# A two-layer graph network on one core: small loads moved to GpSimd's queue, and the order of the first and last pairs laid anew

## The chip, the cores and the metric

The kernel runs on one core of a Trainium2 chip. The core has five engines with a queue of instructions each: TensorE (PE, matrix products), VectorE (DVE), ScalarE (ACT), GpSimd (POOL) and SyncE (SP, which here only issues transfers). The time is device microseconds of one execution; the median of the runs before is 2428.2 us (three runs, 2427.8 to 2429.03). Profiled executions are recorded engine by engine, with the TensorE clock that was granted (1.00 is full speed).

## The reference

x is 128 images (graphs) of 128 nodes with 512 features, float32; adj is one 128 x 128 matrix of zeros and ones for all of them.

```python
def _L0_gnn_ref(x, adj, Wq, bq, Wk, bk, Wv, bv, Wo, bo):      # 8 heads of 64
    q = (x @ Wq + bq).reshape(b, n, H, HD)                    # k and v likewise
    scores = einsum('bqhd,bkhd->bhqk', q, k) / sqrt(HD)
    scores = scores + (1.0 - adj)[None, None, :, :] * -1000000000.0
    attn = softmax(scores, axis=-1)
    out = einsum('bhqk,bkhd->bqhd', attn, v).reshape(b, n, d)
    return out @ Wo + bo

def _L1_gnn_ref(x, W, a, beta, mask):
    h = einsum('bnc,cf->bnf', x, W)
    s1 = einsum('bnf,f->bn', h, a1); s2 = einsum('bnf,f->bn', h, a2)
    e = leaky_relu(s1[:, :, None] + s2[:, None, :], 0.2) * mask[None, :, :]
    att = softmax(e, axis=2)
    return elu(einsum('bij,bjf->bif', att, h) + beta * h)

x = layernorm(x + _L0_gnn_ref(x, adj, ...))
x = layernorm(x + _L1_gnn_ref(x, W, a, beta, adj))
```

## The kernel before

**Pairs.** The 128 images are worked on two at a time, 64 pairs (`G = 2`, `NG = 64`). For each pair the two images are the columns of one 2 x 2 block product: q, k, v, the output product w and the product h of the second layer are each formed by seven block products instead of eight (`product(name, g, n)` with n from 1 to 7), from sums of blocks of the weights (`weight_sum`, formed once at the start) and of the data (`block_sum`, on GpSimd for each pair). Products 1 and 2 need plain blocks alone; the others need sums. A product of q or k is four matmuls of 128 x 128, one of v, w or h two of 128 x 256; as float32 each matmul stands in the trace as two passes. Partial results are taken from PSUM by ScalarE (`take_part`, `take_block`, with the bias `bq_c` or `bk_c`) and by VectorE (`add_block`).

**Stages of a pair.** `fetch_blocks` loads x in blocks (tile xblk, four transfers of 32 partitions), `turn_x` transposes it on VectorE into xT, `block_sum` makes tx; then the products of q and k, `scores` on TensorE, `mask` and `row_max` on VectorE, `exps` and `normalise` on ScalarE. The attention weights are written to DRAM and read back in another layout (`attn_write`, `attn_read`, both on SyncE's queue) and transposed on VectorE (`turn_attn`); then `attend` with v, the product w, to which x + bo is added (`fetch_x`, `residual` on GpSimd), the normalisation, the small attention of the second layer, the product h, elu, the second normalisation and `store`. For the last pair the products w and h are plain ones (`plain`), for which the upper halves of wo and w1 are loaded again into the tiles of wq and wk (`load_again`).

**The order.** Nothing is scheduled automatically. Each step is entered with a number, its place (`at(place, fn, ...)`); all steps are sorted by place and issued in that order (the last three lines of the function). Places of a pair are relative to `g * STEP`, with `STEP = 37.33`; `rows(g)` lists the steps with their usual places, `other` replaces the places of pairs 0 to 3 and of three of the last ones, and `last_rows(g)` has the last pair's own list. The steps that are run once (`weight_sum`, `make_mask`, `make_beta`, `wa_column`, `wa_turn`, `wa_centre`, the loads of wo and w1) have places of their own at the end. An engine works through its instructions in the order of the places, and waits for whatever an instruction needs.

**The loads at the start.** What is issued before the sorted steps stands at lines 119 to 159: four transfers of pair 0's xblk and four of wq, two of each on SyncE's and two on ScalarE's queue; four of wk and four of wv on SyncE's; then eight small ones on ScalarE's queue: the columns bq_c, bk_c and bv_c (128 partitions x 4 single elements), adj, beta broadcast to all partitions, the two halves of a1 broadcast (tile uf, 128 x 512) and bo broadcast (128 x 512). Afterwards `make_identity` builds ident on GpSimd, and `keep_busy(20, "early")` issues 20 matmuls of ident with itself, whose result nobody reads.

**Completion counters.** Transfers issued by SyncE and ScalarE take turns on eight completion counters; a transfer whose counter was used before waits, on its queue, until the transfer that used it last has landed. Transfers issued by GpSimd have eight counters of their own; the kernel before issues none there.

**Who needs what.** The table load ahead of ScalarE's first eviction, and the eviction, need bq; `make_mask` needs adj; `wa_column(j, c)` multiplies a block of w1 by a half of a1 (VectorE, eight of them), from which `wa_turn` and `wa_centre` make two rows that `row_product` uses; `residual` needs bo; `attend_evict` needs bv.

Of the kernel before, what the change touches and what calls it, by code (L numbers as in the profile page):

```python
# [8 lines left out]
F32 = mybir.dt.float32  # L9
AF = mybir.ActivationFunctionType  # L10
ALU = mybir.AluOpType
AX = mybir.AxisListType

P = 128
# [4 lines left out]
STEP = 37.33  # L19
# [3 lines left out]
def gnn_two_layers(  # L23
# [34 lines left out]
    nc = tc.nc  # L58
# [49 lines left out]

    def broadcast(pool, src, n, name):
        t = pool.tile([P, n], F32, tag=name, name=f"{name}_in")  # L110
        nc.scalar.dma_start(out=t, in_=src.rearrange("(o n) -> o n", o=1).broadcast_to([P, n]))
        return t

    def column(src, name):
        t = cpool.tile([P, NC], F32, tag=name, name=name)
        nc.scalar.dma_start(out=t, in_=src.rearrange("(c p) -> p c", p=P))
        return t
# [6 lines left out]
    bq_c = column(bq, "bq_c")  # L124
    bk_c = column(bk, "bk_c")
    adj_sb = cpool.tile([P, N], F32, tag="adj_sb", name="adj_sb")
    nc.scalar.dma_start(out=adj_sb, in_=adj)
    bv_c = column(bv, "bv_c")
    beta_b = broadcast(cpool, beta, 1, "beta_b")
    a_b = [  # L130
        broadcast(wk2, a1[j * D : (j + 1) * D].rearrange("f o -> (f o)"), D, "uf")
        for j in range(2)
    ]
    bo_b = broadcast(cpool, bo, D, "bo_b")
# [24 lines left out]
    nc.gpsimd.memset(mhalf, -0.5)  # L159

# [8 lines left out]
    def make_beta():  # L169
        nc.vector.tensor_scalar(beta_i, ident, beta_b, None, ALU.mult)  # L170
# [6 lines left out]
    def wa_column(j, c):  # L177
        t = wk2.tile([P, D], F32, tag="u", name=f"wa_t_{j}_{c}", bufs=1)
        nc.vector.scalar_tensor_tensor(
            t, w1_sb[:, c, :], 1.0, a_b[j], ALU.mult, ALU.mult,  # L180
            accum_out=wa_col[:, j, c : c + 1],
        )
# [255 lines left out]
    def residual(b):  # L438

        xr[b] = xn.pop(b)  # L440
        nc.gpsimd.tensor_tensor(xr[b], xr[b], bo_b, ALU.add)  # L441
# [25 lines left out]
    def attend_evict(b):  # L467

        oT[b] = wk2.tile([P, NC, N], F32, tag="oT", name=f"oT_{b}")
        nc.vector.tensor_tensor(  # L470
            oT[b], po.pop(b),
            bv_c.rearrange("p (m o) -> p m o", o=1).broadcast_to([P, NC, N]), ALU.add,
        )
# [247 lines left out]
    def last_rows(g):  # L721
        b0, b1 = g * G, g * G + 1
        return (
            (-59.639, fetch_blocks, g), (-24.809, turn_x, g, 0), (-24.149, turn_x, g, 1),
            (-23.429, product, "q", g, 1), (-23.349, block_sum, "x", g, 1),
            (-22.314, take_part, "q", g, 1, 0, 0), (-19.649, block_sum, "x", g, 2),
            (-18.909, block_sum, "x", g, 4), (-18.469, fetch_x, b0),
            (-18.169, block_sum, "x", g, 3), (-18.019, fetch_x, b1),
            (-16.444, product, "q", g, 2), (-15.549, product, "q", g, 7),
            (-15.019, residual, b0), (-14.924, add_block, "q", g, 0, 0, 2, 1),  # L730
            (-14.654, product, "k", g, 7), (-12.889, product, "k", g, 1),
            (-11.994, product, "k", g, 2), (-10.519, take_part, "k", g, 1, 0, 0),
            (-9.799, residual, b1), (-9.379, add_block, "k", g, 0, 0, 2, 1),
            (-9.359, product, "q", g, 6), (-8.244, take_part, "q", g, 6, 1, 0),
            (-8.214, product, "k", g, 6), (-7.319, product, "q", g, 5),
            (-6.769, take_part, "k", g, 6, 1, 0), (-6.109, take_part, "q", g, 5, 1, 1),
            (-5.554, product, "k", g, 5), (-4.649, add_block, "q", g, 1, 1, 7, 5),
            (-3.789, product, "q", g, 4), (-3.349, take_part, "k", g, 5, 1, 1),
            (-2.894, product, "q", g, 3), (-2.649, add_block, "q", g, 1, 0, 4, 6),
            (-2.229, add_block, "k", g, 1, 1, 7, 5), (-1.999, product, "k", g, 3),  # L740
            (-1.779, take_block, "q", g, 0, 1), (-1.104, product, "k", g, 4),
            (-0.884, take_block, "k", g, 0, 1), (0.011, add_block, "k", g, 1, 0, 4, 6),
            (0.661, scores, b0), (1.781, product, "v", g, 1), (2.001, mask, b0, 0),
            (2.671, mask, b0, 1), (2.871, take_part, "v", g, 1, 0, 0), (3.341, row_max, b0),
            (4.201, scores, b1), (4.801, exps, b0, 0), (5.441, mask, b1, 0),
            (5.591, exps, b0, 1), (6.111, mask, b1, 1), (6.781, row_max, b1),
            (6.971, exps, b0, 2), (7.761, exps, b0, 3), (8.691, row_inv, b0),
            (9.141, exps, b1, 0), (9.551, product, "v", g, 7), (9.931, normalise, b0, 0),
            (10.531, normalise, b0, 1), (11.131, normalise, b0, 2), (11.291, product, "v", g, 2),
            (11.731, normalise, b0, 3), (12.381, add_block, "v", g, 0, 0, 2, 1),  # L750
            (12.471, attn_write, b0), (13.891, exps, b1, 1), (14.681, exps, b1, 2),
            (15.471, exps, b1, 3), (15.621, attn_read, b0), (15.641, product, "v", g, 6),
            (16.661, row_inv, b1), (16.731, take_part, "v", g, 6, 1, 0),
            (17.111, normalise, b1, 0), (17.381, product, "v", g, 5), (18.091, normalise, b1, 1),
            (18.691, take_part, "v", g, 5, 1, 1), (19.071, normalise, b1, 2),
            (19.581, add_block, "v", g, 1, 1, 7, 5), (19.671, normalise, b1, 3),
            (19.991, product, "v", g, 3), (20.001, turn_attn, b0, 0), (20.411, attn_write, b1),
            (20.861, product, "v", g, 4), (21.081, take_block, "v", g, 0, 1),
            (21.081, turn_attn, b0, 1), (22.441, add_block, "v", g, 1, 0, 4, 6),
            (23.001, attend, b0), (23.561, attn_read, b1), (25.321, attend_evict, b0),  # L760
            (26.141, plain, "w", b0), (27.801, turn_attn, b1, 0), (29.291, turn_attn, b1, 1),
            (29.951, plain_take, b0), (30.091, attend, b1), (31.301, attend_evict, b1),
            (32.801, plain, "w", b1), (33.361, row_product, b0, 0), (34.091, row_product, b0, 1),
            (34.821, bn_stats, y, b0, "c"), (35.511, bn_aggr, b0, "c"),
            (35.711, add_eps, g, "c", 0), (36.301, inv_std, g, "c", 0), (37.141, plain_take, b1),
            (37.801, scale_s, g, 0), (37.971, bn_stats, y, b1, "c"), (38.861, bn_aggr, b1, "c"),
            (39.061, add_eps, g, "c", 1), (39.231, row_product, b1, 0),
            (39.731, spread_s2, g, 0), (39.961, inv_std, g, "c", 1), (40.381, edge, g, 0),
            (40.711, norm_c, b0), (41.241, row_product, b1, 1), (41.971, scale_s, g, 1),
            (42.141, leaky, g, 0), (42.411, edge_max, g, 0), (42.681, norm_c, b1),  # L770
            (42.821, edge_exp, g, 0), (43.021, spread_s2, g, 1), (43.221, keep_busy, 6, "late"),
            (43.631, edge, g, 1), (43.961, leaky, g, 1), (44.231, edge_max, g, 1),
            (44.501, edge_inv, g, 0), (44.641, edge_exp, g, 1), (44.671, weights, g, 0),
            (45.391, turn_weights, g, 0), (45.691, edge_inv, g, 1),
            (45.811, weights_evict, g, 0), (45.861, weights, g, 1), (46.331, turn_weights, g, 1),
            (46.531, aggregate, b0), (46.751, weights_evict, g, 1), (47.451, aggregate, b1),
            (48.041, aggregate_evict, b0), (48.631, aggregate_evict, b1),
            (48.771, plain, "h", b0), (52.221, plain, "h", b1), (52.771, elu_exp, b0),
            (55.511, elu_max, b0), (55.891, elu_exp, b1), (56.201, elu_sum, b0),
            (56.891, elu_max, b1), (57.581, bn_stats, u, b0, "f"), (58.271, elu_sum, b1),  # L780
            (58.961, bn_aggr, b0, "f"), (59.161, add_eps, g, "f", 0),
            (59.331, bn_stats, u, b1, "f"), (59.471, inv_std, g, "f", 0),
            (60.021, bn_aggr, b1, "f"), (60.221, add_eps, g, "f", 1), (60.391, shift, g, 0),
            (60.531, inv_std, g, "f", 1), (60.731, norm_f, b0), (61.411, shift, g, 1),
            (61.651, store, b0), (61.751, norm_f, b1), (62.671, store, b1),
        )
# [5 lines left out]
            3.605, 8.805, 9.465, 11.005, 14.385, 10.265, 15.125, 11.405, 13.415, 16.725, 12.3,  # L792
# [204 lines left out]
```

## Time and profile before

| | us |
|---|---|
| median of three runs | 2428.2 |
| the profiled execution | 2425.9 |
| its span in the trace | 2424.1 |
| first slice of 40 (60.6 us): busy TensorE / VectorE / ScalarE / GpSimd, tenths | 7 / 4 / 3 / 4 |
| TensorE without work from 60 to 320 us | 4.6 |
| the same from 320 to 2280 us | 1.4 |
| the same from 2280 to 2386 us | 2.5 |
| the same from 2386 us to the end, 2424.1 | 10.2 |
| last matmul ends at | 2415.6 |

The page gives for each engine its busy time and its share of the span; the order of time of an engine gives start and duration of groups of instructions, and in brackets how long the engine was idle before and what ended that. `SPq` and `ACTq` are the issues of transfers on a queue. A view by windows gives, for each stretch of time, the busy time of each engine, the granted clock, the busy share of the 16 DMA engines and the rate. Between 320 and 2280 us a pair takes 36.98 us, and TensorE has work nearly all the time. The loads of the first 60 us, with their size and the time from issue to landing:

```profile
wk_sb<-in_L_gnn_Wk_dram SPq DMA_DIRECT2D x4, 256.0 KB, 7.6
wv_sb<-in_L_gnn_Wv_dram SPq DMA_DIRECT2D x4, 256.0 KB, 9.3
w_sb<-in_L_gnn_W_dram SPq DMA_DIRECT2D x1, 1024.0 KB, 8.8
wo_sb<-in_L_gnn_Wo_dram SPq DMA_DIRECT2D x1, 1024.0 KB, 11.3
uf_in<-in_L_gnn_a_dram ACTq DMA_DIRECT2D x2, 256.0 KB, 5.5
bo_b_in<-in_L_gnn_bo_dram ACTq DMA_DIRECT2D x1, 256.0 KB, 8.4
adj_sb<-in_adj_dram ACTq DMA_DIRECT2D x1, 64.0 KB, 7.3
bq_c<-in_L_gnn_bq_dram ACTq DMA_DIRECT2D x1, 2.0 KB, 8.5
bk_c<-in_L_gnn_bk_dram ACTq DMA_DIRECT2D x1, 2.0 KB, 7.6
```

### The profile page before, as it was taken

The page shows a single profiled execution, that of the slowest core. Times are in us where ns is not written, and L with a number is a line of the kernel's source. Part 1 is how long each engine was busy: PE and PEld are TensorE (multiplying, and loading weights), DVE is VectorE, ACT ScalarE, POOL GpSimd, SP SyncE. Part 2 cuts the span into 40 slices and gives each one's busy share as a digit, 9 for nine tenths or more (in the row PEclk, how much of TensorE's full clock was granted, in tenths as well). Part 3 has the DMA queues.
Part 4 walks back from the last instruction along what each step waited for, and adds up shares of the span by engine and source line. Part 5 has one row for each costly group of instructions (what it writes and reads, how often), then busy time and mean ns, then how long its engine had stood idle before and what let it go on. Part 6 is the DMA issues. An engine that isn't in the chain of part 4 may idle for free.

```text
span 2424.1 us, 50042 instructions
## 1 busy us (share of the span) xinstructions
PE 2389.7 (99%) x17956; PEld 2205.0 (91%) x17956; DVE 1912.0 (79%) x4385; ACT 1488.4 (61%) x5310; POOL 854.8 (35%) x1037
## 2 busy tenths in 40 slices
PE   7999999999999999999999999999999999999998
PEld 6998999999999999999999999999999999999985
DVE  4787787787877877878878778778778787787787
ACT  3665656656666566566566665665665666656655
POOL 4333323423333333234233333332342333333322
PEclk8999999999999999999999999999999999999999
DMA  6324234233242342342332433423424324334331
GB/s 162 119 74 114 79 105 120 75 112 105 82 119 93 92 123 80 105 121 73 113 104 81 122 93 91 123 80 105 119 75 113 106 79 122 92 92 123 88 105 70
DMA packets 204536, 245.30 MB, mean 101 GB/s; under 512 B 20480, under 2 KB 151680, under 8 KB 204288
## 3 DMA queue, kind: packets, MB, share of 16 engines
q1 hardware_dynamic: 201152, 240.46, 34.0%
q8 instruction: 142, 2.33, 0.4%
q10 hardware_dynamic: 3136, 1.65, 0.3%
q14 instruction: 106, 0.87, 0.1%
HBM read 141.37 MB, written 100.66 MB: 100 GB/s over the span
## 4 chain that ended last, share of the span: by engine, by line
PE 92%; DVE 3%; DMA 2%; ACT 1%; SPq 1%; issue 1%; POOL 0%; ACTq 0%; DVEq 0%; POOLq 0%
PE pw L293 11%; PE pk L299 11%; PE pv L293 11%; PE ph L293 11%; PE pq L299 11%; PE eq L299 9%; PE psc L385 5%; PE po L460 5%; PE pz L595 5%; PE ev L293 4%; PE ew L293 4%; PE eh L293 4%; PE pat L582 1%; DMA xblk<-in_x_dram 1%; PE pb L539 1%
## 5 line engine op out<-in xcount | busy, mean ns | idle before, releaser
L407 ACT ACTIVATE s<-s,nmax 128x128 f32<-128x128 f32 x1024 | 397.8, 394 | 1.9 <-DVE nmax L401 1.9
L421 ACT ACTIVATE sb<-s,rinv 128x128 f32<-128x128 f32 x1024 | 327.0, 392 | 25.9 <-DVE rinv L414 25.0
L252 POOL TENSOR_TENSOR tw<-oT 128x256 f32<-128x256 f32 x63 | 46.1, 732 | 748.4 <-DVE oT L470 748.4
L441 POOL TENSOR_TENSOR x<-x,bo_b_in 128x512 f32<-128x512 f32 x128 | 164.6, 1296 | 367.4 <-DMA x<-in_x_dram 366.7
L313 ACT ACTIVATE part_q<-pq,bq_c 128x128 f32<-128x128 f32 x384 | 119.1, 361 | 234.5 <-PE pq L299 234.5
L407 ACT ACTIVATION_READ_ACCUMULATOR s<-s,nmax 128x1 f32 x1024 | 197.0, 192 | 0.0
L313 ACT ACTIVATE part_k<-pk,bk_c 128x128 f32<-128x128 f32 x384 | 120.1, 364 | 111.8 <-PE pk L299 61.9
L585 ACT COPY attT<-pat 128x256 f32<-128x256 f32 (+1 forms) x65 | 24.0, 369 | 268.1 <-PE pat L582 268.1
L393 DVE SCALAR_TENSOR_TENSOR s<-psc,amask 128x512 f32<-128x512 f32 x256 | 164.3, 683 | 26.4 <-PE psc L385 26.3
L450 DVE STREAM_TRANSPOSE attnT<-ab 128x512 f32<-128x512 f32 x256 | 179.1, 701 | 4.8 <-DMA ab<-scr 4.6
L510 DVE SCALAR_TENSOR_TENSOR ya<-w,wa_row 128x512 f32<-128x512 f32 x256 | 173.8, 679 | 4.4
L401 DVE TENSOR_REDUCE nmax<-s 128x8 f32<-128x1024 f32 x128 | 156.1, 1220 | 4.4
L323 DVE TENSOR_TENSOR part_w<-pw,x 128x256 f32<-128x256 f32 x189 | 80.0, 424 | 88.0 <-PE pw L293 88.0
L299 PE MATMUL pk<-xT,wk_sb 128*128 128x128 f32 x1024 | 140.3, 280 | 0.0
L299 PE MATMUL pq<-xT,wq_sb 128*128 128x128 f32 x1024 | 135.1, 275 | 2.0 <-DMA wq_sb<-in_L_gnn_Wq_dram 2.0
L293 PE MATMUL pv<-wv_sb,xT 128*128 128x256 f32 x512 | 123.6, 384 | 12.3 <-DMA wv_sb<-in_L_gnn_Wv_dram 12.3
L299 PEld LDWEIGHTS pq<-xT,wq_sb 128*128 128x128 f32 x1024 | 129.4, 192 | 5.5 <-issue 2.1
L309 ACT COPY part_v<-pv 128x256 f32<-128x256 f32 x192 | 69.9, 364 | 104.1 <-PE pv L293 104.0
L299 PEld LDWEIGHTS pk<-xT,wk_sb 128*128 128x128 f32 x1024 | 129.1, 191 | 4.4 <-issue 0.2
L385 PE MATMUL psc<-kT,qT 64*128 64x128 f32 x2048 | 132.3, 279 | 0.0
L414 DVE RECIPROCAL rinv<-rsum 128x8 f32<-128x8 f32 x128 | 25.2, 197 | 134.7 <-ACT s L407 134.7
L385 PEld LDWEIGHTS psc<-kT,qT 64*128 64x128 f32 x2048 | 119.5, 188 | 11.8 <-issue 11.3
(674 smaller groups left out, 6640.4 us busy)
## 6 DMA issues: line engine op xcount, KB each, us to landing
scr<-sb SPq DMA_DIRECT2D x128, 512.0 KB, 2.7
ab<-scr SPq DMA_DIRECT2D x512, 128.0 KB, 3.0
x<-in_x_dram SPq DMA_DIRECT2D x128, 256.0 KB, 5.0
out_dram<-u SPq DMA_DIRECT2D x128, 256.0 KB, 2.1
xblk<-in_x_dram SPq DMA_DIRECT2D x254, 128.0 KB, 5.6
wk_sb<-in_L_gnn_Wk_dram SPq DMA_DIRECT2D x4, 256.0 KB, 7.6
wv_sb<-in_L_gnn_Wv_dram SPq DMA_DIRECT2D x4, 256.0 KB, 9.3
w_sb<-in_L_gnn_W_dram SPq DMA_DIRECT2D x1, 1024.0 KB, 8.8
```

The costliest lines, as they stand in the source:

```text
L293: nc.tensor.matmul(out, b[:, c, :], a[:, c, :], start=first and c == 0, stop=(c == 1), skip_group_check=True,)
L299: nc.tensor.matmul(out[:, m * N : (m + 1) * N], a[:, c, m * P : (m + 1) * P], b[:, c, :], start=first and m == 0 and c == 0, stop=(c == 1) ...
L313: nc.scalar.activation(dst[:, m, :], src[:, m * N : (m + 1) * N], AF.Identity, bias=col)
L385: nc.tensor.matmul(psc[b][j][:, m, :], qT[g][feats, m, rows], kT[g][feats, m, rows], start=True, stop=True,)
L393: nc.vector.scalar_tensor_tensor(s_t[b][:, j * HP : (j + 1) * HP, :], psc[b][j], SCALE, amask.rearrange("p (o n) -> p o n", o=1).broadcast ...
L401: nc.vector.tensor_reduce(nmax[b], s_t[b], AX.X, ALU.max, negate=True)
L407: nc.scalar.activation(s_t[b][:, h, :], s_t[b][:, h, :], AF.Exp, bias=nmax[b][:, h : h + 1], accum_out=rsum[b][:, h : h + 1],)
L421: nc.scalar.mul(sb[b][:, :, h, :], s_t[b][:, h, :].rearrange("p (b c) -> p b c", c=Q), rinv[b][:, h : h + 1],)
L441: nc.gpsimd.tensor_tensor(xr[b], xr[b], bo_b, ALU.add)
L450: nc.vector.transpose(attnT[b].rearrange("p h (a r) -> p a h r", r=Q)[:, rows], ab[b].rearrange("p a (h c) -> p a h c", c=Q)[:, rows],)
L460: nc.tensor.matmul(po[b][j * HD : (j + 1) * HD, m, :], vb[b][:, h * HD : (h + 1) * HD], attnT[b][:, j * HP + m, :], start=True, stop=True,)
L510: nc.vector.scalar_tensor_tensor(z, y[b], 1.0, wa_row[j], ALU.mult, ALU.mult, accum_out=s12[g][:, i, j : j + 1])
```

## The change

The eight small loads leave ScalarE's queue for GpSimd's. Three (bq, bk, adj) are issued there at the start, the first of them ahead of the instruction that finishes ident; the other five become a step of its own, `load_later`, with a place. The places of pairs 0 to 3, of the last four pairs and of the steps that are run once are other numbers; the steps of `rows` are the same.

```diff
     def broadcast(pool, src, n, name):
-        nc.scalar.dma_start(out=t, in_=src.rearrange("(o n) -> o n", o=1).broadcast_to([P, n]))
+        nc.gpsimd.dma_start(out=t, in_=src.rearrange("(o n) -> o n", o=1).broadcast_to([P, n]))
...
     def column(src, name):
-        nc.scalar.dma_start(out=t, in_=src.rearrange("(c p) -> p c", p=P))
+        nc.gpsimd.dma_start(out=t, in_=src.rearrange("(c p) -> p c", p=P))
...
-    nc.scalar.dma_start(out=adj_sb, in_=adj)
-    bv_c = column(bv, "bv_c")
-    beta_b = broadcast(cpool, beta, 1, "beta_b")
-    a_b = [
-        broadcast(wk2, a1[j * D : (j + 1) * D].rearrange("f o -> (f o)"), D, "uf")
-        for j in range(2)
-    ]
-    bo_b = broadcast(cpool, bo, D, "bo_b")
...
+    nc.gpsimd.dma_start(out=adj_sb, in_=adj)
+    later = {}
+
+    def load_later():
+        later["bv"] = column(bv, "bv_c")
+        later["beta"] = broadcast(cpool, beta, 1, "beta_b")
+        for j in range(2):
+            a_j = a1[j * D : (j + 1) * D].rearrange("f o -> (f o)")
+            later["a", j] = broadcast(wk2, a_j, D, "uf")
+        later["bo"] = broadcast(cpool, bo, D, "bo_b")
...
-    at(19.105, load_weight, w1_sb, w1)
-    at(21.705, load_weight, wo_sb, wo)
-    at(26.185, wa_column, 0, 1)
-    at(28.185, wa_column, 0, 2)
...
+    at(16.62, load_later)
+    at(17.22, load_weight, wo_sb, wo)
+    at(19.82, load_weight, w1_sb, w1)
+    at(25.74, wa_column, 0, 0)
+    at(26.46, wa_column, 0, 3)
+    at(31.22, wa_column, 1, 0)
+    at(31.94, wa_column, 1, 1)
+    at(32.66, wa_column, 1, 3)
```

The order that the places give, for the first steps (block products by name and number, those of pair 1 marked):

| engine | before | after |
|---|---|---|
| TensorE | q 1, 2, 7; v 1, 2; q 6; k 1; v 7; k 7, 6; q 5; k 2, 5; q 4, 3; k 3, 4; q 1 (pair 1); scores | q 1, 2, 7; k 1, 2, 7; v 1, 2; k 6; q 6; k 5; q 5; k 3; q 3, 4; k 4; q 1 (pair 1); v 6; scores |
| GpSimd | ident; sums of xT; sums of wv; residuals | bq, ident, bk, adj; sums of xT; bv, beta, a1 twice, bo; sums of wv; a sum of pair 1; residuals |
| VectorE after the first evictions | wa_column (0,1), (0,2), mask of image 0 | wa_column (0,0), (0,3), mask of image 0, row_max, mask of image 1, three more wa_column |

In the last pair the places of the last store are 62.671 before and 62.97 after; the second image's plain products and aggregation now go ahead of the first's, and `load_again` of wk goes ahead of that of wq.

## The prediction, made before the changed kernel was run

> **What bounds the kernel now.** I read the page first, then the order of time of each engine over the first 60 us, then SyncE's waits, then windows. The page says that TensorE is busy 99% of the span, so only time in which it has no work, or a slow clock, can be won.
>
> ```profile
> span 2424.1 us, 50042 instructions
> PE 2389.7 (99%) x17956; PEld 2205.0 (91%) x17956; DVE 1912.0 (79%) x4385; ACT 1488.4 (61%) x5310; POOL 854.8 (35%) x1037
> PE   7999999999999999999999999999999999999998
> ```
>
> Only the first and the last of 40 slices are short of 9. TensorE's order of time (start, duration) shows where the first is lost:
>
> ```profile
> 1.36 7.11 PE L155 MATMUL early<-ident 128*128 128x128 f32 x40 [1.36 <-POOL ident masks.py:199]
> 10.43 2.02 PE L299 MATMUL pq<-xT,wq_sb 128*128 128x128 f32 x16 [1.96 <-DMA wq_sb<-in_L_gnn_Wq_dram]
> 12.29 1.06 PE L299 MATMUL eq<-tx,s_q 128*128 128x128 f32 x8
> 25.66 3.75 PE L293 MATMUL pv<-wv_sb,xT 128*128 128x256 f32 x8 [12.32 <-DMA wv_sb<-in_L_gnn_Wv_dram]
> 47.51 1.03 PE L293 MATMUL pv<-wv_sb,xT 128*128 128x256 f32 x4
> ```
>
> Three products of q (1, 2, 7) run by 13.3; then 12.3 us pass until wv has landed. From 25.66 on TensorE hardly stops again. Why wv is late stands in the queues of SyncE and ScalarE, and in SyncE's waits (total, times, longest):
>
> ```profile
> 3.44 9.86 SPq L104 DMA_DIRECT2D wk_sb<-in_L_gnn_Wk_dram  x4
> 13.34 3.18 SPq L104 DMA_DIRECT2D wv_sb<-in_L_gnn_Wv_dram  x4
> 3.77 0.40 ACTq L116 DMA_DIRECT2D bq_c<-in_L_gnn_bq_dram  x1
> 4.89 0.56 ACTq L116 DMA_DIRECT2D bk_c<-in_L_gnn_bk_dram  x1
> ...
> SPq L104 <- DMA wq_sb<-in_L_gnn_Wq_dram: 5.4, 1, 5.4
> SPq L104 <- DMA bk_c<-in_L_gnn_bk_dram: 3.0, 1, 3.0
> ```
>
> The loads of wk wait for wq and for bk_c, data they do not need: in the program as built, SyncE and ScalarE share eight completion counters, and each transfer from the ninth on waits for the last holder of its counter. The windows (length, busy times, clock, DMA share, GB/s) show what this costs:
>
> ```profile
> 4.00:9.00 5.00, 4.47 (x30) 4.28 (x28) 1.31 (x2) 0.00 (x0) 2.38 (x4) 1.00 0.98 248
> 9.00:15.00 6.00, 2.92 (x24) 2.75 (x24) 2.77 (x4) 1.82 (x3) 0.47 (x1) 1.00 0.66 118
> 15.00:25.50 10.50, 0.00 (x0) 0.00 (x0) 3.52 (x7) 0.09 (x1) 0.00 (x0) 0.58 1.07 233
> 24.00:27.30 3.30, 1.64 (x4) 1.40 (x5) 0.36 (x1) 0.00 (x0) 1.54 (x2) 0.50 1.14 228
> ```
>
> From 9 to 15 us the transfers move 118 GB/s, beside 248 and 233 around it. And after the long pause TensorE's clock is at 0.50, so the eight first v passes take 3.75 us.
>
> **The change, part by part.**
>
> *The equivalent start.* I reckon from where TensorE would have begun, had it run everything without a pause at full clock. Before: 25.66, minus three q products of 0.89 us (a product of q or k advances 0.89 in the chain of waits), 2.67, plus the half-clock loss: v 3.75 against two times 0.865 (47.51's four passes to the next line), 2.02, and the next q product 1.36 against 0.89, 0.47; together 25.5. After: TensorE's order is q 1, 2, 7, k 1, 2, 7, then v 1, 2. So with Tv for the landing of wv, six products are done by then: Tv - 5.34, plus what the clock takes (0 to 2.5).
>
> *Tv.* Removed from ScalarE's queue: eight small loads (issues 0.3 to 1.05 us each, 4.0 in all, in time in which ScalarE has nothing else to do: nothing won). The first eight shared transfers are now xblk and wq; wk's four follow as xblk lands (VectorE's first transpose at 5.07), wv's four as wq lands (8.6 to 10.4). Bytes up to wv: xblk 0.52 MB, three weights 3.15, adj 0.07, and 0.79 for the two halves of a1 and bo, which GpSimd issues straight after its four sums of pair 0 (ending 9.5) and which therefore still share the way: 4.53 MB. Filling the hole of 9 to 15 us (6 us at 240 instead of 118 GB/s) is worth 3.0 us, and 1.8 us more come from xblk of pair 1 no longer moving ahead of wv's last part (2 to 25.5 us moved 4.96 MB, so 0.43 MB of it). Tv = 25.5 - 4.8 = 20.7; if the 0.79 MB come behind wv, another 3.3 less, 17.4. I take 19.5, nearer to the first, since GpSimd is free at 9.5. Gain: 25.5 - (19.5 - 5.3) = 11.3.
>
> *The clock.* k 1, 2, 7 need wk: 2.7 MB at 250 GB/s from 2.0, about 13.5; they end near 16.2, and the pause until 19.5 is 3.3 us. Before, the clock fell at about 16.6 (0.94 on the mean from 13.6 to 17.0, 0.50 after), 3.3 us after the last product. Costs 0 or 2.5; taken 0.5.
>
> *GpSimd's queue.* No DMA on it is in the trace. Three loads (bq, bk, adj) stand before the sums of pair 0, five (bv, beta, a1 twice, bo) between those and the sums of wv. Bounds for what one holds POOL: the issue rows of the other queues, 0.31 to 1.05 us; or until it lands, 4.1 to 8.5 us, mean 6.5 (52 us for eight). A 512-wide sum takes 1.28 us on POOL and 0.69 on VectorE, so an issue of 0.5 would be 0.9 there: I take 1 us, nearest to the issue rows. The first one now also delays ident, behind which the 20 warming matmuls wait: covered by the 1.96 us pause before 10.43. The five others, 5 us from 9.5, are covered by the wait for wv; at Tv the three sums of wv that v 6 needs take 3.9 us, and TensorE wants them at Tv + 9.75 (v 1 and 2 1.73, eight products 7.1, pair 1's q 1 0.9). So POOL costs nothing up to 2.7 us a load ((29.3 - 3.9 - 3.8) / 8). ScalarE's first eviction now waits for bq from this queue, with 10 us to spare.
>
> The Trainium skill, DMA: Bandwidth & Descriptors, Issuing engines are not separate DMA queues, speaks against the change: loads from SyncE, ScalarE and GpSimd end on the same 16 DMA engines and only issue time is saved. By it alone the sum would be the reordering, 5 us; the 118 GB/s window says that here the way was not full. SBUF — State Buffer, Who interferes with whom, adds that a DMA issued from GpSimd can stall while VectorE runs certain two-port instructions; no run here shows it, and by it the POOL price would be above 1 us.
>
> *What is late next.* w1. VectorE has two wa_column (w1 times a1) ahead of the mask of image 0. On SyncE's queue wo now goes ahead of w1 and x of image 1 ahead of that of image 0, else the order of the first pairs' loads stays. w1's load waits for wv's last quarter and lands some 11 us after Tv (before, the two 1 MB loads landed 8.8 and 11.3 us after issue). From there VectorE must do 11.1 us of rows (five wa_column of 0.73, four mask halves at 0.65, two maxima at 1.22, one 0.2, two adds 0.42, two transposes 0.69) before pair 2's first product, which TensorE reaches at Tv + 21.2: 1 us of stall, 0 to 4, one for one with w1.
>
> *Places.* They set only the order: a pair takes 37.0 us on TensorE in the middle, while the code spaces pairs 37.33. Pairs 0 to 2: from 60 to 320 us TensorE lacks 4.6 us (260 less 255.4); a new order can give these back or double them; taken 0. The last four pairs: 2.5 us lacking from 2280 to 2386, and 10.2 in the last 38.1, of which 8.5 (from 2415.6) are the closing chain, whose steps are the same in either order. The last store's place moves from 62.67 to 62.97, so no gain is claimed: plus or minus 4, taken 0.
>
> Sum: 11.3 - 0.5 - 1 = 9.8. The profiled execution was 2425.9 us, 1.8 around its span; the median is 2428.2, 2.3 above it. Taking the sum off the median gives **2418 us** (span about 2414).
>
> **Rivals.**
> 1. *Later loads take the place of wv.* wo and w1 run at 233 GB/s (15 to 25.5 us) instead of the 390 to 410 that the slices between 28 and 33 us show: 2.1 MB in 9 instead of 5.3 us, so 4 us more stall: 2422. For it: VectorE has no slack there. Against: those two loads ran fast before.
> 2. *The way was full anyway*, wv lands at 25.5 as before. What is left is k ahead of v, 2.7 us, and perhaps the clock, 2.5, less 1 for w1: 2424 to 2426. For it: the same bytes. Against: the 118 GB/s.
> 3. *Slower: GpSimd's queue becomes the bound.* If a load holds POOL as long as the landings, wv's sums are ready at 0.9 + 8 x 6.5 + 2.9 + 3.9 = 60 us, TensorE wants them at 29: 30 us of stall against 11 won, 2447. It decides from (29.3 + 9.8 - 7.7) / 8, 3.9 us a load. For it: bq and bk are 512 rows of 4 bytes each. Against: no issue row above 1.05 us.
> 4. *The new order of the last pairs costs* 6 us or more: 2424.
>
> **How the numbers follow.** Forecast 0.60 (2411 to 2423); rival 1 0.16, rival 2 0.13, rival 3 0.06, rival 4 0.05. A measurement of this kernel tells 0.2% (4.9 us) from no change, so faster is below 2423.3: all of the forecast, 0.13 of rival 1, 0.04 of rival 2, 0.02 of rival 4, 0.79; slower is rival 3 and a little of 4, 0.07; the same 0.14. Range 2410 to 2426: below, Tv of 17.4 (2 more) with 4 to 6 of the places; above, rivals 1, 2 and 4.
>
> **What would show it.** Right: wk's and wv's issues without the 5.4 and 3.0 us waits and all out by about 10.5; over 200 GB/s from 9 to 15 us; wv's first product between 17 and 21 us behind three k products; clock 1.00 from 10 us on; POOL's sums of wv right at its landing. Wrong: wv's first product after 23; POOL still issuing when wv has landed; TensorE waiting on VectorE's transposes near 40 us for more than 4 us; or more than 15 us without TensorE in the last 140 us.

## The result, and the profile of the changed kernel

| | before | changed | ratio (95% interval) |
|---|---|---|---|
| median, first comparison, us | 2428.0 (6 runs) | 2418.8 (6 runs) | 0.9964 (0.9951 to 0.9977) |
| median, on the chip of the second series below, us | 2430.1 (25 runs) | 2425.0 (11 runs) | 0.9977 (0.9969 to 0.9986) |
| profiled execution / its span, us | 2425.9 / 2424.1 | 2418.3 / 2416.6 | |
| TensorE without work, 60 to 320 us | 4.6 | 1.8 | |
| the same, 320 to 2280 us | 1.4 | 2.1 | |
| the same, 2280 to 2386 us | 2.5 | 2.1 | |
| the same, 2386 us to the end | 10.2 | 9.8 | |

The changed kernel is faster, by 9.2 us in the first comparison and by 5.1 in the second: 0.4 and 0.2%, with 1 outside both intervals. First TensorE at the start, the view in order of time (start, duration, group, in brackets the idle time before it and what ended that):

```profile
11.69 2.02 PE L303 MATMUL pq<-xT,wq_sb 128*128 128x128 f32 x16 [1.40 <-DMA wq_sb<-in_L_gnn_Wq_dram]
13.55 1.06 PE L303 MATMUL eq<-tx,s_q 128*128 128x128 f32 x8
16.36 2.02 PE L303 MATMUL pk<-xT,wk_sb 128*128 128x128 f32 x16 [1.75 <-DMA wk_sb<-in_L_gnn_Wk_dram]
18.22 1.06 PE L303 MATMUL eq<-tx,s_k 128*128 128x128 f32 x8
23.57 3.75 PE L297 MATMUL pv<-wv_sb,xT 128*128 128x256 f32 x8 [4.29 <-DMA wv_sb<-in_L_gnn_Wv_dram]
```

Three products of k now fill part of the pause, but wv's first product still starts at 23.57 us (25.66 before), and its eight passes still take 3.75 us: the granted clock was 0.50 from 22.4 to 29.2 us. SyncE's queue (issues, then its waits: total, times, longest) and the windows (length, busy times, clock, DMA share, GB/s) say why:

```profile
3.94 3.07 SPq L104 DMA_DIRECT2D wk_sb<-in_L_gnn_Wk_dram  x4
9.04 3.25 SPq L104 DMA_DIRECT2D wv_sb<-in_L_gnn_Wv_dram  x4
12.90 3.65 SPq L85 DMA_DIRECT2D xblk<-in_x_dram  x4
```

```profile
SPq L104 <- DMA wq_sb<-in_L_gnn_Wq_dram: 3.6, 2, 2.0
SPq L85 <- DMA wk_sb<-in_L_gnn_Wk_dram: 2.9, 4, 0.9
SPq L104 <- DMA xblk<-in_x_dram: 1.3, 1, 1.3
```

```profile
9.00:15.00 6.00, 4.20 (x36) 3.85 (x34) 2.77 (x4) 1.47 (x3) 3.31 (x6) 1.00 1.08 223
15.00:25.50 10.50, 4.85 (x29) 4.36 (x30) 3.57 (x7) 0.63 (x2) 1.82 (x2) 0.85 1.08 237
```

The waits of wk for wq (5.4) and for bk_c (3.0) have become shorter ones, wk's and wv's issues are out by 7.0 and 12.3 us, and from 9 to 15 us 223 GB/s move instead of 118. From there on the transfers run at a steady 223 to 237 GB/s until wv has landed: the way is full, and pair 1's xblk, issued at 12.9 us as wk's parts land, now shares it with wv. GpSimd's queue (issues stand in its own order of time):

```profile
1.32 0.93 POOL L117 DMA_DIRECT2D bq_c<-in_L_gnn_bq_dram  x1 [0.34 <-issue]
2.35 0.30 POOL masks.py:199 TENSOR_SCALAR_AFFINE_SELECT ident<-ident 128x128 f32<-128x128 f32 x1
2.60 0.79 POOL L117 DMA_DIRECT2D bk_c<-in_L_gnn_bk_dram  x1
...
10.70 1.08 POOL L112 DMA_DIRECT2D uf_in<-in_L_gnn_a_dram  x2
...
23.60 1.28 POOL L219 TENSOR_TENSOR s_v<-wv_sb 128x512 f32<-128x512 f32 x1 [11.29 <-DMA wv_sb<-in_L_gnn_Wv_dram]
```

An issue holds GpSimd 0.54 to 0.93 us, and its sums of wv start at wv's landing. The rest of the gain is not at the start at all. This is TensorE of the kernel before near 225 us, when pairs 3 to 6 are in work:

```profile
226.49 1.13 PE L293 MATMUL ph<-w_sb,th 128*128 128x256 f32 x4 [1.66 <-ACT part_h L309]
...
239.80 1.16 PE L299 MATMUL pq<-xT,s_q 128*128 128x128 f32 x8 [1.33 <-DVE qT L371]
```

and the same two groups of the changed kernel, without a bracket, that is without a wait:

```profile
220.41 1.03 PE L297 MATMUL ph<-w_sb,th 128*128 128x256 f32 x4
...
230.02 1.07 PE L303 MATMUL pq<-xT,s_q 128*128 128x128 f32 x8
```

As a measure of progress I take when the scores of each pair start on TensorE. Against the kernel before, the changed one leads by 4.2 us at pair 0 (37.29 against 41.48), 5.0 at pair 5, 8.8 at pair 6, 8.0 at pair 9, 7.0 at pair 61 and 8.0 at the last product. The spans differ by 7.5 us, since what follows the last product takes 9.0 us instead of 8.5. So the two traces put 4 to 5 us at the start, some 3 between pairs 5 and 9, and some 0.5 at the end; 1.0 is lost in the middle.

### The profile page after: what moved, and what is told of

It is laid out like the page before. It is cut to its first block, busy times and chain, and to the rows that moved or that the text cites. A ratio compares the mean times of both kernels' runs of the same rounds, so it can differ in the third digit from the quotient of the medians.

```text
span 2416.6 us, 50056 instructions
## 1 busy us (share of the span) xinstructions
PE 2390.7 (99%) x17956; PEld 2206.0 (91%) x17956; DVE 1910.6 (79%) x4385; ACT 1487.9 (62%) x5310; POOL 860.6 (36%) x1045
## 5 line engine op out<-in xcount | busy, mean ns | idle before, releaser
L425 ACT ACTIVATE sb<-s,rinv 128x128 f32<-128x128 f32 x1024 | 327.0, 392 | 25.7 <-DVE rinv L418 20.3
L397 DVE SCALAR_TENSOR_TENSOR s<-psc,amask 128x512 f32<-128x512 f32 x256 | 164.6, 683 | 25.7 <-PE psc L389 25.7
L464 PE MATMUL po<-attnT,v 128*64 128x128 f32 x2048 | 127.0, 276 | 1.3 <-DVE attnT L454 1.3
L599 PEld LDWEIGHTS pz<-attT,x 128*128 128x128 f32 x1024 | 124.3, 192 | 4.1 <-ACT attT L589 0.5
## 6 DMA issues: line engine op xcount, KB each, us to landing
wv_sb<-in_L_gnn_Wv_dram SPq DMA_DIRECT2D x4, 256.0 KB, 11.1
```

What stands on the lines that cost most here:

```text
L397: nc.vector.scalar_tensor_tensor(s_t[b][:, j * HP : (j + 1) * HP, :], psc[b][j], SCALE, amask.rearrange("p (o n) -> p o n", o=1).broadcast ...
L425: nc.scalar.mul(sb[b][:, :, h, :], s_t[b][:, h, :].rearrange("p (b c) -> p b c", c=Q), rinv[b][:, h : h + 1],)
L464: nc.tensor.matmul(po[b][j * HD : (j + 1) * HD, m, :], vb[b][:, h * HD : (h + 1) * HD], attnT[b][:, j * HP + m, :], start=True, stop=True,)
L599: nc.tensor.matmul(pz[b][:, c, :], x1[b][:, c * P : (c + 1) * P], attT[g][:, i, :], start=True, stop=True,)
```

## The experiments

Two theories stood at the beginning. One: some 4 us come from the start, mostly from k ahead of v, and nearly 4 from the new places of pair 3. The other: the gain comes from the loads' queue, and the stall near 225 us was only an effect of when the first loads arrived. All times below are medians, each ratio is to the kernel before on the same chip.

**1. The queue alone** (queue_alone): the kernel before, its places kept, with the changed kernel's loads.

```diff
+    at(15.86, load_later)
     at(15.865, weight_sum, "v", 3, nc.gpsimd)
```

> The kernel before with only the small loads moved to GpSimd's queue, three ahead of the sums of pair 0 and five ahead of the sums of wv, all places as before. Theory A (start 4 us, of which the places are the larger part; pair 3's places 3.8 us): wv's first product about 2 us earlier than 25.66, the stall near 225 us is still there, total 2425 to 2427, 1 to 3 us faster than before. Theory B (the queue is what pays): 7 us or more faster than before, 2419 to 2421.

Measured: 2429.0 against 2429.8 us, ratio 0.9998 (0.9989 to 1.0007). Its TensorE at the start:

```profile
12.36 1.06 PE L303 MATMUL eq<-tx,s_q 128*128 128x128 f32 x8
22.58 3.62 PE L297 MATMUL pv<-wv_sb,xT 128*128 128x256 f32 x8 [9.17 <-DMA wv_sb<-in_L_gnn_Wv_dram]
```

wv's product came 3 us earlier than in the profile of before, yet the time is the same. Run 4 explains that: before's own loads bring it at 22.7 there too. Theory B (7 us or more) falls, and the 0.8 us between the medians, which the interval doesn't tell from 0, are less than theory A had allowed.

**2. The places alone** (places_alone): the changed kernel, with the small loads on ScalarE's queue at the front again.

```diff
-        nc.gpsimd.dma_start(out=t, in_=...)        # broadcast, column, adj
+        nc.scalar.dma_start(out=t, in_=...)
...
-    at(16.62, load_later)
```

> The changed kernel's places with the small loads on ScalarE's queue again, as before. Theory A (some 4 us of the gain come from the start, most of it from k 1, 2, 7 running ahead of v, and 3.8 us from the new places of pair 3, which remove a stall near 225 us): 2421 to 2423, so 5 to 7 us faster than the kernel before, with wv's first product at 25 to 26 us and no stall near 225 us. Theory B (the loads' queue is what pays, the places are worth nothing): within 1.5 us of the kernel before, about 2428.

Measured: 2422.8 us, ratio 0.9974 (0.9965 to 0.9984), no stall near 225 us. The places bring, without the queue, as much as the whole change, within the intervals. Its TensorE at the start:

```profile
19.34 3.73 PE L303 MATMUL pk<-xT,wk_sb 128*128 128x128 f32 x16 [6.86 <-DMA wk_sb<-in_L_gnn_Wk_dram]
...
23.79 1.89 PE L297 MATMUL pv<-wv_sb,xT 128*128 128x256 f32 x8
```

wv's first product started behind the k products without a pause, earlier than expected. k waits 3 us longer for wk than in the changed kernel (19.34 against 16.36) and runs at half clock (3.73 us), but v then runs at full clock (1.89).

**3. Pair 3's tail put back** (pair3_back): one line of numbers in the changed kernel, among them h 3 and h 4.

```diff
-            92.94, 98.465, 99.555, 100.075, 113.34, 116.45, 114.43, 117.62, ...
+            97.556, 98.231, 99.321, 100.051, 99.996, 101.761, 101.086, 104.101, ...
```

> The changed kernel with pair 3's tail in the order it had before (h products early again). Theory A: the stall near 225 us comes back, 3 to 4 us slower than the changed kernel, 2422 to 2423, and the lead over the kernel before at pair 6 falls from 8.8 to about 5 us. Theory C (the stall near 225 us was an effect of when the loads of the first pairs arrived, so the start took it away): the same as the changed kernel within 1 us, about 2418.5.

Measured: 2425.7 us, ratio 0.9983 (0.9974 to 0.9992). That is 1.5 to 4.6 us slower than the changed kernel, as one goes by its ratio in the second or the first comparison, so the trace has to decide. The stalls are back in its TensorE:

```profile
220.70 1.13 PE L297 MATMUL ph<-w_sb,th 128*128 128x256 f32 x4 [1.39 <-ACT part_h L313]
...
234.03 1.16 PE L303 MATMUL pq<-xT,s_q 128*128 128x128 f32 x8 [1.35 <-DVE qT L375]
```

From pair 5 to pair 6 it takes 41.4 us (before 41.0, changed 37.1). Theory C falls: the start was the changed one, and the stall came all the same.

**4. Pair 3's tail alone** (pair3_alone): the kernel before with the changed kernel's line of numbers for pair 3.

> The kernel before with the changed kernel's places of pair 3 and nothing else. Theory A (the tail of pair 3 ran its h products too early and made the stall near 225 us): 3 to 4.6 us faster than before (ratio 0.998 to 0.9985), the 1.66 and 1.34 us gaps of TensorE at 225 and 238 us gone. Theory C (the stall belongs to the arrival of the first loads): within 1 us of before.

Measured: 2426.2 us, ratio 0.9979 (0.9970 to 0.9988); 37.7 us from pair 5 to 6. The gap at 225 us is gone, and 0.48 us of the one at 238 is left. The next pair takes 0.8 us longer in every kernel with this tail (38.06 to 38.11 against 37.24), so the net in the traces is 40.8 - 37.3 - 0.8 = 2.7 us (from pair 5 to 6, means of the four kernels with the old and the ten with the new tail). This kernel has before's start, and its windows and TensorE correct the picture of that start:

```profile
9.00:15.00 6.00, 2.92 (x24) 2.75 (x24) 3.52 (x7) 1.91 (x3) 0.59 (x1) 1.00 0.92 194
```

```profile
22.70 3.63 PE L293 MATMUL pv<-wv_sb,xT 128*128 128x256 f32 x8 [10.24 <-DMA wv_sb<-in_L_gnn_Wv_dram]
```

With the same loads in the same order as before, 194 GB/s move from 9 to 15 us, not 118, and wv is there at 22.7, not 25.7. The profiled execution on which the prediction was built had a start 3 us later than this one; why, no view shows.

**5. The later small loads behind wv** (late_small).

```diff
-    at(16.62, load_later)
...
     at(20.62, weight_sum, "v", 3, nc.gpsimd)
+    at(20.63, load_later)
```

> The changed kernel with the five later small loads (bv, beta, two halves of a1, bo: 0.79 MB) issued behind GpSimd's first sum of wv, so that they no longer share the way with wv. Theory A (the DMA way is full at 225 to 240 GB/s until wv has landed): wv's first product about 3.3 us earlier, near 20.2 us instead of 23.57, TensorE's clock perhaps held at 1.00: 3 to 5.5 us faster than the changed kernel, 2413 to 2416. Rival D (a load's own queue delivers it at a rate of its own, whatever else moves): wv's first product stays at 23.5, total 2418 to 2419.

Measured: 2424.0 us, ratio 0.9975 (0.9966 to 0.9984), not faster than the changed kernel (0.9964 and 0.9977). The mechanism held, the gain did not. TensorE, then VectorE:

```profile
20.89 1.97 PE L297 MATMUL pv<-wv_sb,xT 128*128 128x256 f32 x8 [1.43 <-DMA wv_sb<-in_L_gnn_Wv_dram]
...
29.64 1.13 PE L303 MATMUL eq<-tx,wq_sb 128*128 128x128 f32 x8 [1.25 <-DVE qT L375]
...
45.73 0.48 PE L297 MATMUL ev<-wv_sb,tx 128*128 128x256 f32 x1 [2.21 <-DVE v L375]
```

```profile
28.87 0.29 DVE L174 TENSOR_SCALAR beta_i<-ident,beta_b_in 128x128 f32<-128x128 f32 x1 [2.14 <-DMA beta_b_in<-in_L_gnn_beta_dram]
29.08 0.42 DVE L375 TENSOR_TENSOR qT<-eq,part_q 128x256 f32<-128x256 f32 x1
...
35.24 1.63 DVE L183 SCALAR_TENSOR_TENSOR wa_t<-w_sb,uf_in 128x512 f32<-128x512 f32 x1
```

With 0.79 MB out of the way wv came 2.7 us earlier (3.3 expected at 238 GB/s) and its passes ran at full clock (1.97). Then beta, now late, held VectorE in front of qT, and VectorE's rows of w1 and a1 (`wa_column`) held v: 3.5 us went back. These five rows took 1.09 to 1.63 us each, 6.7 together, because GpSimd was adding at the same time; rows of this kind without an addition beside them take 0.68 (more on this in run 8). Rival D falls.

**6. The clock held** (keep_clock): 16 unused matmuls between k and v.

```diff
+    at(14.4, keep_busy, 16, "gap")
     at(15.14, make_mask)
```

> The changed kernel with 16 idle matmuls between the k products and wv's first product. If the clock's fall during the 4.3 us pause costs what the trace says (3.75 instead of 1.9 us for the eight v passes): v still starts at 22.6 to 23.6, the passes take 1.9 us, pair 0's scores come 2 us earlier, and 1.5 to 2.2 us are won, unless VectorE's rows between 36 and 46 us are then late, as they were with the later small loads (stall 2.2 us there); then 0 to 1 us.

Measured: 2424.8 us, ratio 0.9974 (0.9965 to 0.9984), beside 0.9977 for the changed kernel in the same series. TensorE:

```profile
20.30 3.74 PE L145 MATMUL gap<-ident 128*128 128x128 f32 x32
23.87 1.89 PE L297 MATMUL pv<-wv_sb,xT 128*128 128x256 f32 x8
...
87.94 1.61 PE L464 MATMUL po<-attnT,v 128*64 128x128 f32 x16 [2.50 <-DVE attnT L454]
```

The passes took 1.89 us as expected, and pair 0's scores came 1.0 us earlier (35.10 against 36.07). The lead was given back in the next pairs: TensorE waits 0.73 us at 58 us, where the changed kernel does not, and at 85 us 2.50 instead of 1.26 for VectorE's attnT, behind which the clock falls once more (po takes 1.61 us instead of 1.09). At pair 5 this trace is 2.7 us behind that of run 8. Between the means 0.3 us are won, plus or minus 2.2.

**7. Only a1 and bo behind wv, w1 ahead of wo** (late_bulk).

```diff
+    def load_last():
         for j in range(2):                  # a1's halves, then bo
...
-    at(17.22, load_weight, wo_sb, wo)
-    at(19.82, load_weight, w1_sb, w1)
+    at(17.22, load_weight, w1_sb, w1)
+    at(19.82, load_weight, wo_sb, wo)
     at(20.62, weight_sum, "v", 3, nc.gpsimd)
+    at(20.63, load_last)
```

> The changed kernel with only a1's halves and bo (0.79 MB) behind GpSimd's first sum of wv; bv and beta stay ahead of the sums, and w1's load goes ahead of wo's on SyncE. In the run with all five later, wv's first product came at 20.89 and the clock held, but TensorE lost 1.25 us at 28.4 (beta landed at 28.9 and VectorE's row of it stood ahead of qT) and 2.21 us at 43.5 (VectorE behind its rows of w1 and a1). Theory: with beta early the first stall is gone and with w1 first the second shrinks to 0 to 1 us: 2 to 4 us faster than the changed kernel. Rival: VectorE's rows of w1 now wait for a1 instead and TensorE loses as much: the same as the changed kernel.

Measured: 2421.6 us, ratio 0.9964 (0.9951 to 0.9976), 3.4 us under the changed kernel's 2425.0 of the same series. TensorE:

```profile
20.64 1.97 PE L299 MATMUL pv<-wv_sb,xT 128*128 128x256 f32 x8 [0.45 <-DMA wv_sb<-in_L_gnn_Wv_dram]
...
42.83 1.13 PE L299 MATMUL ev<-wv_sb,tx 128*128 128x256 f32 x4 [0.83 <-DVE v L377]
```

The first stall of run 5 is gone and 0.83 us of the second is left, as expected. Between the means 3.1 us are won, plus or minus 2.3.

**8. The changed kernel again** (after_again).

> The changed kernel as it is, beside the three others on one chip, as the mark that they are measured against. A ratio to the kernel before of 0.9951 to 0.9977 as in the first comparison; if the changed kernel beats the one with its places alone (ratio 0.9974), the loads on GpSimd's queue are worth something under the new places, and if it lies at 0.997 to 0.998, they are worth nothing.

Measured: 2425.0 us, ratio 0.9977 (0.9969 to 0.9986). Pair 0's scores start at 36.07 (37.29 in the first profile), but from pair 9 to 60 this execution takes 10.4 us longer than the first profile of before, where the first profile of the changed kernel took 1.0 longer. GpSimd, and VectorE at the same time:

```profile
1270.98 1.26 POOL L445 TENSOR_TENSOR x<-x,bo_b_in 128x512 f32<-128x512 f32 x1 [5.17 <-DMA x<-in_x_dram]
```

```profile
1271.07 1.46 DVE L558 SCALAR_TENSOR_TENSOR ee<-ev 128x256 f32<-128x256 f32 x1
...
1273.52 0.38 DVE L375 TENSOR_TENSOR qT<-pq,part_q 128x256 f32<-128x256 f32 x1
```

x lands, GpSimd adds bo, and the row ee, which begins 0.09 us later, takes 1.46 us instead of 0.42. qT is late, and TensorE, which wanted it, stood for 0.36 us. All 18 of its listed waits in the middle (6.4 us) are for this qT. The group of ee between 320 and 2280 us (shortest / median / longest, ns), first profile of the changed kernel, then this one:

```profile
L558 DVE SCALAR_TENSOR_TENSOR ee<-ev x53: 424/425/1527, 340.8 to 2267.7; 128x256 f32<-128x256 f32 x53
```

```profile
L558 DVE SCALAR_TENSOR_TENSOR ee<-ev x53: 424/854/1542, 341.1 to 2277.4; 128x256 f32<-128x256 f32 x53
```

Counted one by one, 7 of the 53 rows are longer than 0.8 us in the first and 27 in this one (before: 6); in this one 36 rows overlap the addition, with a median of 1.20 us, and the 17 that do not take 0.42. The order decides: the 27 long rows all began while the addition ran and ended 0.28 us after it, the 9 others began first and took 0.42. From pair 9 to 60 the 24 pairs without a long row took 36.98 us each, to 0.01; the 27 with one took 13.3 us more in all (in the first profile 7 pairs and 4.0 us, in before's 6 and 2.9). So these rows account for all of the middle's lost time. Whether x lands in front of ee differs from execution to execution, and it blurs every comparison above.

**9 to 12. The addition moved** (quiet_after, quiet_before, quiet_places, quiet_bulk): in the changed kernel, in the kernel before, in run 2's and in run 7's, the two additions of the pairs in the middle go behind GpSimd's sums, where x has long landed.

```diff
-            (0.19, residual, b0), (0.52, add_block, ...), (1.47, residual, b1),
+            (19.00, residual, b0), (0.52, add_block, ...), (19.10, residual, b1),
```

> The changed kernel with GpSimd's two additions of bo to x moved, in the pairs of the middle, from where x lands to behind GpSimd's sums of the pair (place 19 instead of 0.2 and 1.5). In its profile on this series' second chip the middle (pairs 9 to 60) lost 10.4 us against 1 us in the first profile: VectorE's row ee takes 0.42 us alone and 1.2 us beside that addition (36 of 53 pairs; 15 in the first profile, where it seldom lengthened), and each long one makes qT late and stops TensorE for 0.3 to 0.6 us. Theory E (this collision, decided by when x lands, is what separates runs of one kernel): no long ee is left, the pairs advance 36.98 us each, 4 to 8 us faster than the changed kernel's 2425, 2417 to 2421, with less spread between executions. Rival: the addition only collides elsewhere, the same as 2425 within 1.5.

> The kernel before with the same move of GpSimd's additions in the middle. Theory E: 2 to 6 us faster than before, and the difference to the changed kernel with this move is what the change itself is worth without the collisions: by the parts (first pairs' places 3, pair 3's places 4 to 5, the queue 0) 7 to 8 us. If the difference is 9 to 11 instead, the start gains more than the parts say, and if it is under 5, the middle took part of it away.

> The changed kernel's places with the small loads on ScalarE's queue, and the same move. Theory F (GpSimd's queue is worth nothing, since the way is full until wv has landed): the same as the changed kernel with this move, within 1 us. Rival G (under the new places the queue is worth the 3 us that the transfers' 9 to 15 us window would give): 3 us slower than it.

> The changed kernel with a1's halves and bo behind GpSimd's first sum of wv, w1 ahead of wo, and the same move. If the 3.4 us of the first and 4 to 8 us of the second edit add up: 2413 to 2417, the fastest of all.

| 5 executions each | median, us | lowest to highest | ratio (95% interval) |
|---|---|---|---|
| quiet_before | 2420.4 | 2417.1 to 2420.8 | 0.9955 (0.9943 to 0.9968) |
| quiet_places | 2415.2 | 2413.1 to 2415.3 | 0.9935 (0.9922 to 0.9947) |
| quiet_after | 2414.6 | 2413.6 to 2415.7 | 0.9934 (0.9920 to 0.9948) |
| quiet_bulk | 2412.0 | 2411.3 to 2413.0 | 0.9925 (0.9912 to 0.9937) |

The move takes some 10 us off both kernels, more than expected, and the changed kernel's spread falls from 6.6 us (11 executions) to 2.1 (5). The window from 320 to 2280 us, after_again and then quiet_after:

```profile
320.00:2280.00 1960.00, 1953.22 (x14711) 1807.80 (x14711) 1568.08 (x3585) 1224.43 (x4376) 698.89 (x847) 1.00 0.34 101
```

```profile
320.00:2280.00 1960.00, 1960.00 (x14842) 1822.37 (x14841) 1575.20 (x3604) 1231.27 (x4402) 695.64 (x851) 1.00 0.34 101
```

TensorE has no gap left there, and one of the 53 rows ee is still long: theory E holds. Without this noise the change is worth 4.9 us between the means (95%: 3.0 to 6.8), less than the 7 to 8 expected, since the start and pair 3's places are each worth less than the first two profiles had made them (below); and run 7's edit adds 2.6 us (plus or minus 1.1). quiet_bulk is the fastest kernel of the study.

The queue is worth -0.1 us (plus or minus 1.3), so theory F's number holds and rival G falls. Theory F's reason holds only in part. With the loads on ScalarE's queue (run 2, quiet_places) the way was not full: 173 and 183 GB/s from 9 to 15 us, beside 219 to 226 in four kernels with the changed start (the changed one twice, pair3_back, quiet_after). GpSimd's queue brings k's first product from 19.6 to 15.7 us and wv's sums from 24.1 to 23.0 (means). But then TensorE waits between k and v, the clock falls, and v takes 3.05 to 3.75 us instead of 1.89 and 1.97. Pair 0's scores come at 36.2 us with GpSimd's queue and at 35.1 without.

## Why the prediction came out right, and where its steps did not

The number was met (2418 against 2418.8; the ratio of the second comparison, 0.9977, would make it 2422.6, inside the range of 2410 to 2426), but by a sum in which the largest term failed and the places, which were taken as 0, stood in for it. That these met is luck. In the prediction's own reckoning the start of the two profiles comes to 25.5 - (23.57 - 5.34) - 2.8 for the clock = 4.5 us, against 11.3 - 0.5 - 1 = 9.8 in the sum; the measured lead at pair 0 is 4.2. Term by term:

*Tv, taken 19.5, between 17.4 and 20.7.* This step failed: 23.57, 23.27 and 22.56 us in three profiles, outside its bounds. By the prediction's own list, wv's first product after 23 was a sign of being wrong. The 3.0 us for the hole came about (223 instead of 118 GB/s). The fault is in the bytes: it counted 4.53 MB and let pair 1's xblk (0.52 MB) come behind wv, for another 1.8 us. But xblk_1 is issued as wk's parts land, at 12.9 us, and shares the way. (4.53 + 0.52) MB at the measured 238 GB/s from 2 us are 23.2, and 5.08 MB moved in the trace from 2 us until wv landed. Run 5 shows the same from the other side: without 0.79 MB, 2.7 us earlier.

*The start before, 25.5.* Right for the profile at hand, but that execution was an exception: 22.58, 22.70 and 22.59 us in three other executions with before's places. The 118 GB/s, on which 3.0 us of the gain rested, were 194 in the two of them that also have before's loads. So against such a start wv gains nothing, and rival 2's case is what held there: wv no earlier, and of its 2.7 us for k ahead of v 1.8 are seen. Pair 0's scores come at 36.2 instead of 38.0 us (means of four and of three kernels), and 1.4 us are left at pair 5; the new places bring a wait of 1.27 us for attnT near 87 us that was not there before. k ahead of v was not tried by itself.

*GpSimd's queue, 1 us a load, no cost.* Right: 0.54 to 0.93 us, and hidden where the prediction said. Rival 3 had no ground. But no time was gained by it either (queue_alone, quiet_places). The prediction named the Trainium skill, DMA: Bandwidth & Descriptors, Issuing engines are not separate DMA queues, by which only issue time is saved, and let the 118 GB/s decide against it. The runs agree with the page. In before's order the queue has SyncE's issues of wv out by 11.1 us instead of 14.3 (queue_alone, pair3_alone) and moves 220 instead of 194 GB/s from 9 to 15 us, but the lead is gone by 22.5: 237 against 245 GB/s from 2 us on, wv's product at 22.58 against 22.70, the time 2429.0 against 2429.8 us.

*The clock, 0.5, between 0 and 2.5.* Too small: it fell, as in before, and stayed low until 29.20. Two products of v and two of k and q took from 23.57 to 29.90, 6.3 us, instead of 3.5 by the prediction's 0.865 and 0.89 a product: 2.8 us, above the bound. k came late as well: it began at 16.36, not by 13.5 (2.7 MB at 250 GB/s from 2.0 us are in fact 12.8), and the pause behind it was 4.3 us instead of 3.3. Before loses nearly as much, but its 2.5 are in the 25.5 already, so the sum should have had the whole 2.8 here.

*w1 next, 1 us.* w1 landed 10.5 us after wv (taken 11), and with wv at 23.5 there was no stall. Run 5, with wv at 20.9, has one of 2.21 us, but there the rows of w1 and a1 took 6.7 us instead of five times 0.73, which alone is more than the stall. So the wait was seen in the right place, and the prediction's price for the rows was too low; what w1's lateness costs by itself is not shown. Rival 1 is not seen either: 329 GB/s from 24.0 to 27.3 us.

*Places of pairs 0 to 3, taken 0, bounds 4.6.* This is the term that made up for it: 2.7 us net from pair 3's tail, inside the bounds. Before, TensorE reached product h of pair 3 while ScalarE's part_h was not there. The prediction saw the 4.6 us that were lacking from 60 to 320 us and did not look where they stood: three of them were the two waits at 225 and 238 us, and the diff moved just that tail.

*The end, taken 0.* Right: from pair 61's scores to the last product 131.9 us (mean of four kernels with before's end) and 131.3 (ten with the new one), but what follows takes 8.5 and 8.9, so 140.5 and 140.2 to the end of the span: 0.2 us, within the scatter of the ten (138.9 to 141.2). Rival 4 is not seen. Not tried by itself.

Together 1.4 + 2.7 + 0.2 = 4.3 us, beside the 4.9 (3.0 to 6.8) measured without the noise; with before's late start counted among the others the first term is 2.3 and the sum 5.2. The 9.2 of the first comparison are these and, by its interval (5.6 to 11.9), in part chance: in its traces the start of before was some 3.8 us later at pair 5 than in the three other kernels with that start. Whether that late start was usual for the six executions of before in that comparison is open, as only one was profiled.

## What to carry to other kernels

Before a gap in one profile is priced, see whether a second execution has it: here 3 us of a start and up to 10 us of the middle were matters of the single execution. When a wait for a load is to be shortened, count every transfer that can be issued before it lands, also those that the change itself sets free, and divide by the rate of the full way. Changing the issuing queue brought wk 4 us forward here, wv by 1 us at most, and the kernel by nothing. And where TensorE stops for well under a microsecond again and again, look for another engine's row that is longer than its twins, and at who ran beside it.

## What the runs showed of the hardware

A VectorE row with two inputs in SBUF stands still while GpSimd adds from SBUF: ee 0.42 us alone, a median of 1.20 beside the addition, 1.46 in the example, where it ended 0.3 us after the addition did. Over the 14 traces of this study, between 320 and 2280 us, each of the 192 rows ee over 0.8 us began while an addition of bo was running; the 112 in which one began took 0.42 to 0.43, and that addition up to 1.55 instead of 1.27. Rows beside it with one input in PSUM (qT, 0.38 to 0.42) or a transpose (0.70) did not lengthen. The Trainium skill, SBUF — State Buffer, Who interferes with whom, says just this: with two SBUF inputs VectorE contends with a GpSimd instruction that reads SBUF, and the order of issue decides which one blocks. The prediction had used that section for the DMA issues only, which stayed under the 1 us taken (0.54 to 0.93).

The granted clock changes in steps of 3.41 us: in the changed kernel it is 1.00 from 8.72 to 22.37 us (four steps) and 0.50 until 29.20 (two). TensorE's idle time within one step goes with the clock of the next: 1.98 us (after_again, 13.85 to 15.83), 2.21 (run 5) and 2.50 (run 6) were followed by half clock, 1.70 (quiet_bulk, 18.82 to 20.52) was not. Over the 14 traces all 25 falls follow a step with 1.98 us or more idle, and no step with up to 1.79 was followed by one; a single step with 2.02 (quiet_after, 2403.61 to 2407.02) kept the clock, so the bound is near 2 us and not sharp. At half clock, a step with 1.20 us idle (the changed kernel, 22.37 to 25.78) was followed by another at half clock, one with 0.50 (after_again, 17.16 to 20.57) by one at full clock.

The eight small loads were 2,304 packets of ScalarE's queue (3,136 before, 832 after) and are 400 on GpSimd's; so many fewer did not make wv land earlier.
